# One drain a step in place of raises on PE's products, in a message-passing layer of a graph network

## The chip, the core and the metric

The kernel runs on one core of a Trainium2 chip. It has five engines with a queue each, which work side by side: PE (TensorE) multiplies matrices, DVE (VectorE) and ACT (ScalarE) do elementwise work, POOL (GpSimd) here issues gathers, and SP (SyncE) issues other transfers. An engine waits for another by a semaphore, which an instruction raises when it completes. The metric is the device time of one execution in microseconds. PE's granted clock is listed by the profile as a share of full speed.

## The reference

The inputs are 12,500 nodes `x` with 128 numbers each, and 400,000 edges with a source, a destination (sorted) and a distance. What is computed, cut to what matters:

```python
rbf = exp(-(d[:, None] - centers) ** 2 / (2 * width * width))   # 50 centers
cut = 0.5 * (cos(pi * d / 10) + 1) * (d <= 10)
W = (silu(rbf @ fw1 + fb1) @ fw2 + fb2) * cut[:, None]
messages = (h[src] @ pw + pb) * W
agg = segment_sum(messages, dst, num_segments=num_atoms)
h1 = h + (silu(agg @ mw1 + mb1) @ mw2 + mb2)
out = layernorm(x + h1, axis=-1)
```

The distances are scaled so that most edges lie beyond the cutoff and contribute nothing.

## The kernel before

**Stages.** First the nodes are projected (`h @ pw + pb`) into a table `proj` in HBM, four blocks of 128 at a time (helpers at L1003, L345, L348), while the edges are packed in seven chunks: DVE drops those beyond the cutoff and lists source, destination and factor of the rest. Then a loop goes over 139 quads of edges; a quad is four tiles of 128 edges, 512 in all. The steps 0 to 131 stand in one loop, the last ones are written out by hand. Node blocks are finished in between, as soon as their edges have been summed, and later chunks are still packed in the first steps.

**One step q of the loop.** The order in which the code names the operations is the order of each engine's queue:

- `message(q)`, DVE, L1201: the filter of quad q (a PSUM bank `pu`) times the gathered rows gives `msg`, 128 x 512.
- `nodes(q)`: work on finished node blocks; `node_first` (PE L1282, L1283, then ACT L1285 into `zs`), `node_second` (PE L345, L348), statistics (DVE L1320, L1324), normalisation (ACT L1371).
- Gathers of the rows of later quads, POOL, L1099, four a quad. A table PACE says at which count of DVE's vector instructions each is issued, so they are spread among DVE's work.
- `second(q + 2)`, PE, L1182 and L1185: bias and four products with `fw2` into a bank.
- In steps with q%4 of 0 and 1: `first(octs(q))`, PE, L1167, two products of 512 columns into `ph`, and `silu(octs(q))`, ACT, L1173, from `ph` into `s`. One such pair serves two quads, four and five or six and seven steps after the group's first; `ph` is a single buffer of two banks, `s` has three.
- In steps with q%4 of 3: two `basis`, ACT, L1151 (square) and L1155 (exponential), into `rbf` (two buffers). Silu and exponential need different tables, so ACT loads a table ahead of the first of each pair.
- `sum_up(q)`, PE, L1235: four products of `msg` with the column matrices `hot` into `sums`, two PSUM buffers for two quads each.
- `place(q + 1)`, DVE, L1214: four column matrices `hot` of the next quad, from destinations and cutoff factors. `msg` and `hot` have two buffers up to quad 65, four from 66 on (`own`).
- `add`, DVE, L1269: the sums of an earlier pair of quads are added into `aggT` at an address that is loaded first (L1244).

An fp32 product runs on PE as two passes, so one product of L1185 or L1235 stands as two instructions in the profile, with a weight load each.

**What sets the waits.** A scheduler finds for each instruction what it depends on, and gives it a wait on the semaphore of the engine that made it. Any product of PE that somebody waits for raises PE's semaphore (PE_49 in the listings below). The tiles `rbf`, `ph` and `s` are taken from a pool that turns their buffers.

Of the kernel before, what the change touches and what calls it, by code (L numbers as in the profile page):

```python
# [29 lines left out]
QT = 4  # L30
# [25 lines left out]
OTHERS = 4, 5, 6, 7  # L56
OWN_4 = 66
DIRECT = 32
FIRST = 16
LISTS = 5  # L60
PACE = ((2, 17), (3, 26), (4, 36), (5, 54), (7, 95), (9, 125), (10, 144), (12, 170), (18, 250), (24, 324), (30, 373), (36, 458), (42, 544), (48, 612), (54, 691), (60, 754), (66, 826), (72, 902), (78, 982), (84, 1071), (90, 1139), (96, 1218), (102, 1306), (108, 1357), (114, 1414), (120, 1461), (126, 1518), (132, 1580), (138, 1646), (139, 1666))
# [30 lines left out]
def kernel(  # L92
# [288 lines left out]
        return max([int(DONE[0] * max(p - s, 0) ** 2) - 1] + [n for k, n in LAST.items() if p >= k])  # L381
    proj = nc.dram_tensor("proj", [N, H], F32).ap()
    near_d = nc.dram_tensor("near_d", [NP, 2 * P], F32).ap()

    free = [ps.tile([P, 512], F32, name=f"bank{k}", bufs=1) for k in range(4)]
    held = []
# [445 lines left out]
    def unpack(c):  # L832
# [14 lines left out]
            listed(pair, a, b, 0, 3)  # L847
        if c < 2:
            more_ = np_ if c == 0 else SPILL
            also = work.tile([P, 2, QE], F32, name="s", bufs=3).bitcast(I32)  # L850
            listed(also, 0, more_, 3, LISTS)
        awake[c] = max(awake[c], clock[0]) + (6 if c < 1 else 3.5 if c < 2 else 4.0)
        yield 0
# [172 lines left out]
        free.append(b)  # L1026


    d_of, rbf_of, ph_of, t_of, s_of, pu_of, got_of, pa_of, hot_of = ({} for _ in range(9))


# [55 lines left out]
    def beside(n):  # L1087

        while n and singles[1]:
            n -= 1  # L1090
            one_row(1)
# [48 lines left out]
    def basis(o):  # L1140
        if o not in d_of:
            for q in quads(o):
                while chunk_of(q) not in stored:
                    go_on(todo[0])
            radials(o + 1)
        d, n = d_of.pop(o)
        u = 2 * KR
        rbf = work.tile([P, QE], F32, name="rbf")
        if o >= 0:
            nc.scalar.wait_ge(d_sem[o % 3], 16 * (o // 3 + 1))  # L1150
        a = nc.scalar.activation(rbf[:u], d[:u], AF.Square, bias=rbf_bias[:u], scale=rbf_scale[:u])  # L1151
        if o >= 0:
            tc.declare_no_dep(a.ins, group="lengths", reason="waits on d_sem")
        beside(HIDE[0])
        nc.scalar.activation(rbf[:u], rbf[:u], AF.Exp, scale=-1.0 / (2.0 * width * width))  # L1155
        beside(HIDE[1])
        rbf_of[o] = rbf, n
        if o >= 0:
            based[0] = o + 1
            radials(o + 4)  # L1160

    def first(o):

        rbf, n = rbf_of.pop(o)
        ph = ps.tile([P, 2, QE], F32, name="ph", bufs=1)
        for h in range(n):
            nc.tensor.matmul(ph[:, h, :], w1_sb[:2 * KR, h, :], rbf[:2 * KR], start=True, stop=True)  # L1167
        ph_of[o] = ph, n

    def silu(o):  # L1170
        ph, n = ph_of.pop(o)
        s = work.tile([P, 2, QE], F32, name="s", bufs=3)
        nc.scalar.activation(s[:, :n], ph[:, :n], AF.Silu)  # L1173
        beside(HIDE[2])
        for h in range(n):
            s_of[2 * o + h] = s[:, h]

    def second(q):

        s = s_of.pop(q)  # L1180
        pu = bank()
        nc.tensor.matmul(pu, ones_b[:, :P], bias_b["fb2"].rearrange("k j f -> k (j f)"), start=True,  # L1182
                         stop=False)
        for j in range(QT):
            nc.tensor.matmul(pu[:, j * H:(j + 1) * H], s[:, j * P:(j + 1) * P], fw2_sb,  # L1185
                             start=False, stop=(j == QT - 1))
        pu_of[q] = pu

    def message(q, js=(0, QT)):
        gathers(q + 1)  # L1190
        msg = own(q, "msg", 0)
        a, b = js
        if q in SINGLY and a == 0:
            act = q in BY_ACT
            k = (BY_ACT if act else BY_SP).index(q)
            assert q in alone and all(s[0] != q for s in singles[act])
            nc.vector.wait_ge(row_sem[act][k % ROW_SEMS], 16 * P * (k // ROW_SEMS + 1))
            m = nc.vector.tensor_mul(msg[:, 0, :], pu_of[q][:, :H], alone.pop(q))
            tc.declare_no_dep(m.ins, group="rows", reason="waits on row_sem")
            a = 1  # L1200
        nc.vector.tensor_mul(msg[:, a:b, :], pu_of[q].rearrange("p (j f) -> p j f", j=QT)[:, a:b, :],  # L1201
                             got_of[q][:, a:b, :])
        if b == QT:
            free.append(pu_of.pop(q))
            got_of.pop(q)
        gathers()
        return msg

    def place(q):

        hot = own(q, "hot", 1)
        for j in range(QT):
            at = 2 * q + j // 2, slice(j % 2, j % 2 + 1)
            nc.vector.tensor_scalar(hot[:, j, :wide(q)], iota_n[:, :wide(q)], dl[:, at[0], at[1]],  # L1214
                                    cut[:, at[0], at[1]], op0=OP.is_equal, op1=OP.mult)
            gathers()
        hot_of[q] = hot

# [8 lines left out]
    def sum_up(q, msg, js=range(QT)):  # L1227
        hot = hot_of[q]
        if q % 2 == 0 and 0 in js:
            pa_of["two"] = ps.tile([P, 2, 2 * W], F32, name="sums", bufs=2)  # L1230
        pa = pa_of[q] = pa_of["two"][:, q % 2, :]
        n = QT // windows(q)
        for j in js:
            k = j // n
            nc.tensor.matmul(pa[:, k * W:k * W + wide(q)], msg[:, j, :], hot[:, j, :wide(q)],  # L1235
                             start=(j % n == 0), stop=(j % n == n - 1))

    bases = {}

# [25 lines left out]
    def add(q, ks=(0, 1)):  # L1265
        pa = pa_of[q]
        for k in ks[:windows(q)]:
            to = aggT[:, ds(bases.pop((q, k)), wide(q))]
            nc.vector.tensor_add(to, to, pa[:, k * W:k * W + wide(q)])  # L1269
            gathers()  # L1270
        done[0] = q + (ks[-1] == 1)

# [179 lines left out]

    def keep_busy(n):

        ph = ps.tile([P, 2, QE], F32, name="ph", bufs=1)
        for k in range(n):
            nc.tensor.matmul(ph[:, k % 2, :], ones_b[:, :P],
                             bias_b["mb2"].rearrange("k j f -> k (j f)"), start=True, stop=True)
# [132 lines left out]

    some, counted = None, []
    for q in range(NL - 7):
        while todo and q + 2 >= DIRECT // QT and todo[0] <= chunk_of(min(q + 2, NQ - 1)):
# [12 lines left out]
        radials(q // 2 + 5)  # L1607
        one_by_one()
        multiplies(q + 1 + EARLY_X)
        if q + 2 < NL:  # L1610
            second(q + 2)
        if q % 4 < 2 and 2 * octs(q) < NL:
            first(octs(q))
            silu(octs(q))
        if q % 4 == 3:
            for o in (q // 4 * 2 + 4, q // 4 * 2 + 5):
                if 2 * o < NL and q < NL - 8:
                    basis(o)
        sum_up(q, msg)
        now = range(added(q), added(q + 1))  # L1620
        at_once = len(now) == 2 and wide(now[0]) == wide(now[1]) and windows(now[0]) == windows(now[1])
        if at_once:
            bases_of(list(now))
        else:
            for k in now:
                base_of(k, (0,))
        place(q + 1)
        for k in now:
            if not at_once:
                base_of(k, (1,))  # L1630
            add(k)
        tail(q)
        clock[0] = max(clock[0], there_at[q])
        summed[q] = clock[0] + 0.7
        clock[0] += 2.2 + 0.3 * (windows(q) - 1)
        if q == 0:
            clear_packed(2, nc.sync)
        if todo:
            pack_until(max(there_at[q + 1], clock[0] + (PACK_US if known[0] >= QB[3] else EARLY_US)), NC_)
        if NODES - 8 <= q < NODES - 2:  # L1640
            part_of(*(("mb1", mb1_f) if q < NODES - 5 else ("mb2", mb2_f)), (q - NODES + 8) % 3)
        if not todo and not counted:
            counted.append(q)
            count()
        elif counted and some is None and fetched[0] >= QT * NL and not queue:
            some = nc.values_load(bad_i[0:1, 2:3], min_val=0, max_val=3 * E)
    def house(q):
# [247 lines left out]
```

## Time and profile before

| | us |
|---|---|
| median of three runs | 956.14 |
| the runs | 954.89, 956.14, 960.9 |
| the profiled execution | 950.38 |
| its span | 948.8 |
| PE busy in it | 663.7 |
| POOL busy in it | 539.2 |
| granted clock of PE in it | 0.808 of full speed |

The span is the time from the first to the last instruction of the profiled execution. Rows of groups give line, engine, operation, tile, shape and count, then the busy time in us and the mean of one in ns, then the idle time of the engine ahead of them with what ended it. "remote" there is a wait that ended with a semaphore's event at which the profile finds no instruction of this core that had just ended; in the chain the same is called "another core or an unknown queue". "issue" is time in which an engine waited for nothing that the profile shows. Rows of the timeline give the start, the duration, the engine and line, and in brackets the idle time before.

### The profile page before, as it was taken

The numbers are of one execution on the slowest core, as the hardware profiler recorded it, in microseconds if no ns is written. First come the engines' busy times: TensorE is split into PE (matmuls) and PEld (weight loads), VectorE is DVE, ScalarE is ACT, GpSimd is POOL, SyncE is SP. The second block draws the span as 40 slices with busy tenths as digits, with TensorE's granted clock in tenths as the row PEclk, the third lists the DMA queues.
The fourth block names the chain that finished last, engine by engine and source line by source line (L and its number), as shares of the span: only waits on it lengthen the run. The fifth ranks groups of instructions, "written<-read, shape, count | busy, mean of one in ns | idle before, by whom it ended". The sixth has DMA issues, their size and how long they took to land.

```text
span 948.8 us, 11718 instructions
## 1 busy us (share of the span) xinstructions
PE 663.7 (70%) x3531; PEld 517.3 (55%) x3531; DVE 565.9 (60%) x1725; ACT 398.0 (42%) x567; POOL 539.2 (57%) x577
## 2 busy tenths in 40 slices
PE   4663737749778867767767786868796675777656
PEld 3552535537556755655555564646575554554444
DVE  8356638745778767767678584646553344443536
ACT  4432622316335443534334433634643542454235
POOL 6346355565556656666666465546565566664661
PEclk8677767778778878888978898769987787778778
DMA  7574421232233223232324122432422342232222
GB/s 243 161 222 154 147 96 34 77 92 81 62 79 120 71 62 82 69 108 77 94 64 136 54 68 67 120 100 67 142 63 63 105 122 67 65 111 81 70 75 74
DMA packets 51295, 91.23 MB, mean 96 GB/s; under 512 B 12928, under 2 KB 18656, under 8 KB 51226
## 3 DMA queue, kind: packets, MB, share of 16 engines
q0 software_dynamic: 18096, 37.30, 15.6%
q1 hardware_dynamic: 22868, 35.09, 11.2%
q10 hardware_dynamic: 10262, 18.05, 6.0%
q8 instruction: 29, 0.48, 0.2%
q14 instruction: 40, 0.33, 0.1%
HBM read 74.59 MB, written 15.79 MB: 95 GB/s over the span
## 4 chain that ended last, share of the span: by engine, by line
PE 42%; another core or an unknown queue 16%; issue 13%; DVE 13%; ACT 10%; DVEq 1%; DMA 1%; ACTq 0%
PE ph L1167 11%; PE bank L1185 9%; PE sums L1235 9%; PE bank L348 5%; DVE hot L1214 3%; PE bank L1182 3%; PE bank L1283 2%; DVE msg L1201 2%; ACT s L1173 2%; ACT rbf L1151 2%; PE bank L1003 1%; PE bank L345 1%; ACT rbf L1155 1%; DVE aggT L1269 1%
## 5 line engine op out<-in xcount | busy, mean ns | idle before, releaser
L1099 POOL DMA_INDIRECT quad<-proj,srci x412 | 391.7, 951 | 274.0 <-issue 86.1
L1185 PEld LDWEIGHTS bank<-fw_sb,s 128*128 128x128 f32 x1112 | 177.1, 225 | 90.2 <-issue 83.6
L1173 ACT ACTIVATE s<-ph 128x1024 f32<-128x1024 f32 x70 | 71.2, 1017 | 335.6 <-PE ph L1167 159.9
L1167 PE MATMUL ph<-rbf,w_sb 102*128 102x512 f32 x278 | 164.1, 719 | 51.7 <-ACT s L1173 35.7
L1185 PE MATMUL bank<-fw_sb,s 128*128 128x128 f32 x1112 | 180.1, 310 | 22.5 <-issue 22.2
L1214 DVE TENSOR_SCALAR hot<-iota_n,dl,cut 128x80 f32<-128x80 f32 (+4 forms) x408 | 111.1, 338 | 107.0 <-PE sums L1235 49.6
L1235 PEld LDWEIGHTS sums<-hot,msg 128*128 128x128 f32 x816 | 121.5, 218 | 61.3 <-issue 40.3
L1235 PE MATMUL sums<-hot,msg 128*128 128x80 f32 (+4 forms) x816 | 122.5, 299 | 17.3 <-DVE msg L1201 10.1
L1099 POOL DMA_INDIRECT x<-proj,srci x96 | 91.4, 952 | 66.4 <-issue 21.3
L1167 PEld LDWEIGHTS ph<-rbf,w_sb 102*128 102x128 f32 x278 | 57.3, 229 | 99.7 <-issue 58.8
L1269 DVE TENSOR_TENSOR aggT<-aggT,sums 128x80 f32 (+4 forms) x209 | 53.9, 258 | 94.1 <-remote 33.8
L1182 PE MATMUL bank<-fb_b,ones_b 96*128 96x512 bf16 x139 | 60.3, 434 | 49.6 <-DVE msg L1201 15.2
L1201 DVE TENSOR_TENSOR msg<-bank,quad 128x512 f32<-128x512 f32 x78 | 53.2, 682 | 46.2 <-remote 32.7
L348 PEld LDWEIGHTS bank<-pw_sb,xT 128*128 128x128 f32 (+1 forms) x292 | 47.2, 232 | 59.0 <-issue 40.3
L1099 POOL DMA_INDIRECT quad<-in_x_dram,srci x48 | 46.3, 965 | 33.9 <-issue 12.6
L1235 PE MATMUL sums<-quad,quad 128*128 128x128 f32 (+3 forms) x296 | 49.4, 309 | 15.8 <-issue 15.2
L1151 ACT ACTIVATE rbf<-d_sb,rbf_bias,rbf_scale 102x512 f32<-102x512 f32 x70 | 56.1, 801 | 0.0
L1235 PEld LDWEIGHTS sums<-quad,quad 128*128 128x128 f32 x296 | 45.0, 225 | 20.1 <-issue 18.8
L348 PE MATMUL bank<-pw_sb,xT 128*128 128x128 f32 (+1 forms) x292 | 48.5, 319 | 6.2 <-ACT xT L1005 5.6
L345 PE MATMUL bank<-pb_b,ones_b 96*128 96x512 bf16 (+2 forms) x38 | 16.8, 443 | 46.4 <-ACT xT L1005 29.0
L1201 DVE TENSOR_TENSOR quad<-bank,quad 128x512 f32<-128x512 f32 (+1 forms) x40 | 25.9, 647 | 38.0 <-DMA quad<-proj,srci 24.2
L1005 ACT COPY xT<-bank 128x512 f32<-128x512 f32 (+1 forms) x37 | 21.3, 580 | 63.5 <-remote 49.0
(278 smaller groups left out, 881.7 us busy)
## 6 DMA issues: line engine op xcount, KB each, us to landing
d_sb<-near_d ACTq DMA_DIRECT2D x67, 256.0 KB
x<-in_x_dram SPq DMA_DIRECT2D x46, 256.0 KB
quad<-proj,srci POOLq DMA_INDIRECT x412
proj<-hp SPq DMA_DIRECT2D x24, 256.0 KB
out_dram<-x SPq DMA_DIRECT2D x22, 256.0 KB
x<-proj,srci POOLq DMA_INDIRECT x96
r_d<-in_edge_weight_dram SPq DMA_DIRECT2D x5, 256.0 KB
r_dst<-in_dst_dram SPq DMA_DIRECT2D x5, 256.0 KB
```

The source lines that it names most:

```text
L345: nc.tensor.matmul(to[:m, a:a + c, :], ones_b[:, :m], bias_b[:, :c, :], start=True, stop=False)
L348: nc.tensor.matmul(to[:m, k, :], lT[:, k * P:k * P + m], w, start=False, stop=(k == a + c - 1))
L1099: g = nc.gpsimd.indirect_dma_start(out=got[:, j, :], out_offset=None, in_=proj if table is None else table, in_offset=bass.IndirectOffsetO ...
L1151: a = nc.scalar.activation(rbf[:u], d[:u], AF.Square, bias=rbf_bias[:u], scale=rbf_scale[:u])
L1167: nc.tensor.matmul(ph[:, h, :], w1_sb[:2 * KR, h, :], rbf[:2 * KR], start=True, stop=True)
L1173: nc.scalar.activation(s[:, :n], ph[:, :n], AF.Silu)
L1182: nc.tensor.matmul(pu, ones_b[:, :P], bias_b["fb2"].rearrange("k j f -> k (j f)"), start=True, stop=False)
L1185: nc.tensor.matmul(pu[:, j * H:(j + 1) * H], s[:, j * P:(j + 1) * P], fw2_sb, start=False, stop=(j == QT - 1))
L1201: nc.vector.tensor_mul(msg[:, a:b, :], pu_of[q].rearrange("p (j f) -> p j f", j=QT)[:, a:b, :], got_of[q][:, a:b, :])
L1214: nc.vector.tensor_scalar(hot[:, j, :wide(q)], iota_n[:, :wide(q)], dl[:, at[0], at[1]], cut[:, at[0], at[1]], op0=OP.is_equal, op1=OP.mult)
L1235: nc.tensor.matmul(pa[:, k * W:k * W + wide(q)], msg[:, j, :], hot[:, j, :wide(q)], start=(j % n == 0), stop=(j % n == n - 1))
L1269: nc.vector.tensor_add(to, to, pa[:, k * W:k * W + wide(q)])
```

## The change

From step 4 on the products of `first`, `second` and `sum_up` are left out of the scheduler's dependences and raise nothing. Behind each step's `sum_up` PE gets a `drain` that raises a semaphore `products` by one: 128 of them, for the steps 4 to 131. Those who read what the products wrote, or write what the products read, wait for a count of that semaphore, an engine only once for each count. `message(q)` waits for the drain of step q - 2, where its `second` was issued. `place(q + 1)` waits for the drain of the last step that read the buffer. `add` waits for the later step of its pair, `basis` for step q - 2. `silu` is moved behind `sum_up` and the drain, and waits for the drain of its own step. Since dependences are no longer tracked on them, `s`, `rbf` and `ph` become fixed buffers taken in turn. The node blocks, the packing, the projection and the steps written by hand keep their raises. In the built programs the products that raise fall from 601 to 251. PE's order of products is the same.

```diff
+    pe_sem = tc.alloc_semaphore("products")
+    step_q, waited = [-1], {}
+
+    def drained():
+
+        d = nc.tensor.drain()
+        d.then_inc(pe_sem, 1)
+        tc.no_tile_sem_insts.add(d.ins.name)
+
+    def product(i):
+
+        if step_q[0] >= FROM_DRAIN:
+            tc.add_to_no_dep_group("products", i.ins)
+
+    def behind(eng, q):
+
+        n = q - FROM_DRAIN + 1
+        if step_q[0] < 0 or n <= 0:
+            return False
+        if n > waited.get(str(eng.engine), 0):
+            waited[str(eng.engine)] = n
+            eng.wait_ge(pe_sem, n)
+        return True
+
+    def no_word(i, on=True):
+
+        if on:
+            tc.declare_no_dep(i.ins, group="products", reason="the engine waited on pe_sem")
...
     def silu(o):
         ph, n = ph_of.pop(o)
-        s = work.tile([P, 2, QE], F32, name="s", bufs=3)
-        nc.scalar.activation(s[:, :n], ph[:, :n], AF.Silu)
+        s = in_turn_of("s", [P, 2, QE], 3)
+        known_q = behind(nc.scalar, step_q[0])
+        no_word(nc.scalar.activation(s[:, :n], ph[:, :n], AF.Silu), known_q)
...
     def message(q, js=(0, QT)):
         gathers(q + 1)
         msg = own(q, "msg", 0)
         a, b = js
+        known_q = behind(nc.vector, q - 2)
...
     def place(q):
 
         hot = own(q, "hot", 1)
+        known_q = behind(nc.vector, q - (4 if q >= OWN_4 + 4 else 2))
...
             to = aggT[:, ds(bases.pop((q, k)), wide(q))]
-            nc.vector.tensor_add(to, to, pa[:, k * W:k * W + wide(q)])
+            known_q = behind(nc.vector, min(q | 1, step_q[0]))
+            no_word(nc.vector.tensor_add(to, to, pa[:, k * W:k * W + wide(q)]), known_q)
...
             second(q + 2)
         if q % 4 < 2 and 2 * octs(q) < NL:
             first(octs(q))
-            silu(octs(q))
         if q % 4 == 3:
             for o in (q // 4 * 2 + 4, q // 4 * 2 + 5):
                 if 2 * o < NL and q < NL - 8:
                     basis(o)
         sum_up(q, msg)
+        if q >= FROM_DRAIN:
+            drained()
+        if q % 4 < 2 and 2 * octs(q) < NL:
+            silu(octs(q))
```

On ACT a group of four steps reads as follows before; the two silus are those of its first and second step, and L237 clears a piece of `aggT`:

```order
L237 ACTIVATE aggT<-iota_n 128x500 [waits DVE_49]
L1173 ACT_TABLE_LOAD
L1173 ACTIVATE s<-ph 128x1024 [waits PE_49]
L237 ACTIVATE aggT<-iota_n 128x500
L1173 ACTIVATE s<-ph 128x1024 [waits PE_49]
```

The same place on ACT after the change, where L1173 has become L1217:

```order
L238 ACTIVATE aggT<-iota_n 128x500 [waits DVE_49]
L1217 ACT_TABLE_LOAD [waits products]
L1217 ACTIVATE s_560<-ph_958 128x1024
L238 ACTIVATE aggT<-iota_n 128x500
L1217 ACTIVATE s_961<-ph_958 128x1024 [waits products]
```

The waits of both silus are on the new semaphore, and at the first the wait has moved ahead of the table load; so it stands at 23 of the 32 loads that belong to a changed silu, and at the others between load and silu.

On DVE a step of the chunk whose columns are 112 wide reads as follows before; the message is L1201, the columns L1214, and the two additions L1269, with address instructions between them:

```order
L1201 TENSOR_TENSOR msg_680<-bank_170,quad_84 128x512 [waits DMASW3_49,DMASW4_49,DMASW2_49,DMASW1_49]
L1244 TENSOR_LOAD base_i
L1214 TENSOR_SCALAR hot_1073<-iota_n,dl,cut 128x112 [waits PE_49] x4
L1269 ISA
L1269 TENSOR_TENSOR aggT<-aggT,sums 128x112
L1269 ISA
L1269 TENSOR_TENSOR aggT<-aggT,sums 128x112 [waits DVE_49]
```

The same step on DVE after the change:

```order
L1247 TENSOR_TENSOR msg_680<-bank_170,quad_84 128x512 [waits DMASW3_49,DMASW4_49,DMASW2_49,DMASW1_49]
L1295 TENSOR_LOAD base_i
L1263 TENSOR_SCALAR hot_1069<-iota_n,dl,cut 128x112 [waits products]
L1263 TENSOR_SCALAR hot_1069<-iota_n,dl,cut 128x112 x3
L1321 ISA
L1321 TENSOR_TENSOR aggT<-aggT,sums 128x112
L1321 ISA
L1321 TENSOR_TENSOR aggT<-aggT,sums 128x112 [waits DVE_49]
```

The four column matrices waited each for one product of the sums that had read their slice; now the first waits for a drain and the rest for nothing. Message and additions have no wait of their own on PE at this place, before or after.

More of the change, by code (lines that the diff above doesn't have):

```diff
@@ L58 @@
 DIRECT = 32
+FROM_DRAIN = 4
 FIRST = 16
@@ L383, with in_turn_of @@
     near_d = nc.dram_tensor("near_d", [NP, 2 * P], F32).ap()
+    turn_of = {}
+    def in_turn_of(name, shape, n, pool=keep):
+        k = turn_of[name] = turn_of.get(name, -1) + 1
+        if k < n:
+            turn_of[name, k] = pool.tile(shape, F32, name=f"{name}{k}", bufs=1)
+        return turn_of[name, k % n]
     free = [ps.tile([P, 512], F32, name=f"bank{k}", bufs=1) for k in range(4)]
@@ L849, in unpack @@
             more_ = np_ if c == 0 else SPILL
-            also = work.tile([P, 2, QE], F32, name="s", bufs=3).bitcast(I32)
+            also = in_turn_of("s", [P, 2, QE], 3).bitcast(I32)
             listed(also, 0, more_, 3, LISTS)
@@ L1147, in basis @@
         u = 2 * KR
-        rbf = work.tile([P, QE], F32, name="rbf")
+        rbf = in_turn_of("rbf", [P, QE], 2)
         if o >= 0:
             nc.scalar.wait_ge(d_sem[o % 3], 16 * (o // 3 + 1))
+        known_q = behind(nc.scalar, step_q[0] - 2)
         a = nc.scalar.activation(rbf[:u], d[:u], AF.Square, bias=rbf_bias[:u], scale=rbf_scale[:u])
@@ L1153, in basis @@
             tc.declare_no_dep(a.ins, group="lengths", reason="waits on d_sem")
+        no_word(a, known_q)
         beside(HIDE[0])
-        nc.scalar.activation(rbf[:u], rbf[:u], AF.Exp, scale=-1.0 / (2.0 * width * width))
+        no_word(nc.scalar.activation(rbf[:u], rbf[:u], AF.Exp, scale=-1.0 / (2.0 * width * width)),
+                known_q)
         beside(HIDE[1])
@@ L1164, in first @@
         rbf, n = rbf_of.pop(o)
-        ph = ps.tile([P, 2, QE], F32, name="ph", bufs=1)
+        ph = in_turn_of("ph", [P, 2, QE], 1, ps)
         for h in range(n):
-            nc.tensor.matmul(ph[:, h, :], w1_sb[:2 * KR, h, :], rbf[:2 * KR], start=True, stop=True)
+            product(nc.tensor.matmul(ph[:, h, :], w1_sb[:2 * KR, h, :], rbf[:2 * KR], start=True,
+                                     stop=True))
         ph_of[o] = ph, n
@@ L1181, in second @@
         pu = bank()
-        nc.tensor.matmul(pu, ones_b[:, :P], bias_b["fb2"].rearrange("k j f -> k (j f)"), start=True,
-                         stop=False)
+        product(nc.tensor.matmul(pu, ones_b[:, :P], bias_b["fb2"].rearrange("k j f -> k (j f)"),
+                                 start=True, stop=False))
         for j in range(QT):
-            nc.tensor.matmul(pu[:, j * H:(j + 1) * H], s[:, j * P:(j + 1) * P], fw2_sb,
-                             start=False, stop=(j == QT - 1))
+            product(nc.tensor.matmul(pu[:, j * H:(j + 1) * H], s[:, j * P:(j + 1) * P], fw2_sb,
+                                     start=False, stop=(j == QT - 1)))
         pu_of[q] = pu
@@ L1199, in message @@
             tc.declare_no_dep(m.ins, group="rows", reason="waits on row_sem")
+            no_word(m, known_q)
             a = 1
-        nc.vector.tensor_mul(msg[:, a:b, :], pu_of[q].rearrange("p (j f) -> p j f", j=QT)[:, a:b, :],
-                             got_of[q][:, a:b, :])
+        m = nc.vector.tensor_mul(msg[:, a:b, :],
+                                 pu_of[q].rearrange("p (j f) -> p j f", j=QT)[:, a:b, :],
+                                 got_of[q][:, a:b, :])
+        no_word(m, known_q)
         if b == QT:
@@ L1211, in place @@
         hot = own(q, "hot", 1)
+        known_q = behind(nc.vector, q - (4 if q >= OWN_4 + 4 else 2))
         for j in range(QT):
             at = 2 * q + j // 2, slice(j % 2, j % 2 + 1)
-            nc.vector.tensor_scalar(hot[:, j, :wide(q)], iota_n[:, :wide(q)], dl[:, at[0], at[1]],
+            i = nc.vector.tensor_scalar(hot[:, j, :wide(q)], iota_n[:, :wide(q)], dl[:, at[0], at[1]],
                                     cut[:, at[0], at[1]], op0=OP.is_equal, op1=OP.mult)
+            no_word(i, known_q)
             gathers()
@@ L1234, in sum_up @@
             k = j // n
-            nc.tensor.matmul(pa[:, k * W:k * W + wide(q)], msg[:, j, :], hot[:, j, :wide(q)],
-                             start=(j % n == 0), stop=(j % n == n - 1))
+            product(nc.tensor.matmul(pa[:, k * W:k * W + wide(q)], msg[:, j, :],
+                                     hot[:, j, :wide(q)], start=(j % n == 0),
+                                     stop=(j % n == n - 1)))
     bases = {}
@@ L1453, in keep_busy @@
     def keep_busy(n):
-        ph = ps.tile([P, 2, QE], F32, name="ph", bufs=1)
+        ph = in_turn_of("ph", [P, 2, QE], 1, ps)
         for k in range(n):
@@ L1646 @@
             some = nc.values_load(bad_i[0:1, 2:3], min_val=0, max_val=3 * E)
+    step_q[0] = -1
     def house(q):
```

1 line of the change is left out of this document (added).

## The prediction

> **What bounds the kernel now.** I read the page first: engines, then the chain that ended last.
>
> ```profile
> span 948.8 us, 11718 instructions
> PE 663.7 (70%) x3531; PEld 517.3 (55%) x3531; DVE 565.9 (60%) x1725; ACT 398.0 (42%) x567; POOL 539.2 (57%) x577
> PE 42%; another core or an unknown queue 16%; issue 13%; DVE 13%; ACT 10%; DVEq 1%; DMA 1%; ACTq 0%
> ```
>
> No engine is full. PE carries 42% of the chain, and 16% is time for which the profile finds no cause on this one core. The change lies in the steps of the loop, so I asked for the chain from 165 to 925 us, and for the bias products of `second` (one a step) in that stretch.
>
> ```profile
> by line: another core or an unknown queue 17.4%; PE ph L1167 12.9%; issue 12.5%; PE bank L1185 11.3%; PE sums L1235 10.3%; DVE hot L1214 3.7%; PE bank L1182 3.1%; PE bank L348 2.5%; PE bank L1283 2.3%; DVE msg L1201 2.3%; ACT s L1173 1.8%;
> 165.00:925.00 760.00, 57.02 (x132) 16.97 (x132) 0.82 0.30 85
> ```
>
> 132 steps in 760 us are 5.76 us a step. Of the chain there PE has 12.9 + 11.3 + 10.3 + 3.1 + 2.5 + 2.3 = 42.4%: what I add to PE's time counts, as an estimate, with 0.424. The unexplained 17.4% are 0.174 x 760 = 132 us. The list of waits tells who stands in it (columns: total us, times, longest).
>
> ```profile
> ACT s L1173 <- remote: 109.2, 14, 11.9
> DVE hot L1214 <- remote: 44.9, 18, 5.3
> DVE aggT L1269 <- remote: 33.8, 7, 6.7
> DVE msg L1201 <- remote: 32.7, 6, 8.3
> ```
>
> All four wait for PE's semaphore in the code, so "remote" here is a raise that came when no product of PE had just ended: 14 + 18 + 7 + 6 = 45 times. One of them in the timeline, about 608 us:
>
> ```profile
> 608.68 1.88 PE L1167 MATMUL ph<-rbf,w_sb 102*128 102x512 f32 x4
> ...
> 621.74 0.94 POOL L1099 DMA_INDIRECT quad<-proj,srci  x1 [0.31 <-issue]
> 623.24 1.02 ACT L1173 ACTIVATE s<-ph 128x1024 f32<-128x1024 f32 x1 [11.04 <-remote]
> ...
> 626.19 0.94 POOL L1099 DMA_INDIRECT quad<-proj,srci  x1 [3.51 <-DVE base L954]
> ```
>
> `first` was through at 610.56; its silu began at 623.24, 12.7 us later and 0.6 us behind the end of a gather, after which POOL paused for 3.5 us. So PE's word is late while gathers follow each other. The question on which the forecast turns is whether only the word is late, or the product's completion. A second place says something on that:
>
> ```profile
> 782.01 1.05 PE L348 MATMUL bank<-mw_sb,zs 128*128 128x128 f32 x8
> 782.90 0.38 PE L1182 MATMUL bank<-fb_b,ones_b 96*128 96x512 bf16 x1
> 783.12 1.05 PE L1185 MATMUL bank<-fw_sb,s 128*128 128x128 f32 x8
> 784.01 1.06 PE L1235 MATMUL sums<-quad,quad 128*128 128x128 f32 x8
> 784.91 0.38 PE L1182 MATMUL bank<-fb_b,ones_b 96*128 96x512 bf16 x1
> 785.13 1.18 PE L1185 MATMUL bank<-fw_sb,s 128*128 128x128 f32 x6
> 787.96 0.27 PE L1185 MATMUL bank<-fw_sb,s 128*128 128x128 f32 x1 [1.65 <-issue]
> 790.08 0.37 PE L1185 MATMUL bank<-fw_sb,s 128*128 128x128 f32 x1 [1.85 <-issue]
> 792.18 0.37 PE L1235 MATMUL sums<-quad,quad 128*128 128x128 f32 x1 [1.72 <-issue]
> 793.37 0.94 POOL L1099 DMA_INDIRECT quad<-proj,srci  x1 [0.30 <-issue]
> 794.97 0.37 PE L1235 MATMUL sums<-quad,quad 128*128 128x128 f32 x1 [2.42 <-issue]
> 797.07 1.44 PE L1235 MATMUL sums<-quad,quad 128*128 128x128 f32 x6 [1.73 <-issue]
> ```
>
> From 787.96 PE starts one pass every 2.1 us, waiting for no engine, and runs freely again behind POOL's pause. Between the first L348 pass and the one at 787.96 lie 8 + 1 + 8 + 8 + 1 + 6 = 32 passes. I read this as a window: a pass starts only when the one 32 before it has retired. Those that retired so slowly are then the passes of L348, and the first seven of these raise nothing. So completion itself seems late, raise or not.
>
> **The change, part by part.** In the two programs the products that raise fall from 601 to 251; 128 drains that raise are added, one a step from step 4 to 131. Their order among PE's other instructions is unchanged, as are POOL and SP.
>
> *Raises taken away: 0.* A stretch at full clock shows what a raise costs PE, and gives the prices for the drain and for `silu`:
>
> ```profile
> 499.79 1.08 PE L1235 MATMUL sums<-hot,msg 128*128 128x112 f32 x8
> 500.60 0.11 PEld L1182 LDWEIGHTS <-ones_b 96*128 96x128 bf16 x1
> 500.71 0.38 PE L1182 MATMUL bank<-fb_b,ones_b 96*128 96x512 bf16 x1
> 500.93 1.05 PE L1185 MATMUL bank<-fw_sb,s 128*128 128x128 f32 x8
> 501.82 1.88 PE L1167 MATMUL ph<-rbf,w_sb 102*128 102x512 f32 x4
> 503.54 1.04 PE L1235 MATMUL sums<-hot,msg 128*128 128x112 f32 x8
> 503.74 1.02 ACT L1173 ACTIVATE s<-ph 128x1024 f32<-128x1024 f32 x1 [1.72 <-issue]
> 506.07 1.15 PE L1235 MATMUL sums<-quad,quad 128*128 128x112 f32 x8 [0.38 <-DVE quad L1201]
> 509.39 0.69 DVE L1201 TENSOR_TENSOR quad<-bank,quad 128x512 f32<-128x512 f32 x1
> ```
>
> The eight passes of L1185 take from 500.93 to the start of `first` at 501.82, 0.11 us each, with the raise on the last; the next product follows at the same 0.11 us. So I take 0 for 350 raises. The Trainium skill, TensorE: Matmul & The Clock Gate, section "The cost: per-tile semaphore tail", says that such increments are written one behind the other at about 26.3 ns each; by it 350 fewer would be an estimated 9 us less work, and the sum below about 980 instead of 989. These rows don't show it in PE's pace.
>
> *Drains: +21.* A drain keeps the next product back until the sums have ended. Back to back, L1182 starts at 500.71, 0.16 us before the modelled end of the sums (499.79 + 1.08). Behind a drain this 0.16 is lost; the weight load of 0.11 us, hidden now, stands open; and a group that starts from rest takes 1.15 instead of 1.04, 0.11 more. That is 0.38 us, times 128 = 49 us on PE, times 0.424 = 21. Bounds: 0 where PE waits anyway after the sums, and twice the price at half clock with all of it on the path, 97 us. A drain alone gains nothing. I take the middle since the three parts come from rows of just this place.
>
> *`silu` behind sums and drain: +12.* At 503.74 the silu starts 0.04 us after `first` ended, while the sums run. Now it waits for them (1.04) and the drain. `ph` is one buffer: the next step's `first` must wait for that silu. Half of the silus are preceded by a table load, and in the new order the wait stands ahead of 23 of these loads:
>
> ```profile
> L1173 ACT ACT_TABLE_LOAD x35 | 44.9, 1283 | 0.8 <-issue 0.2
> PE ph L1167 <- ACT s L1173: 35.7, 9, 6.6
> ```
>
> Behind the drain come load and silu, 1.28 + 1.02 = 2.30 us; PE has only `second` to fill it, 501.82 - 500.71 = 1.11. PE stands 1.2 us, 23 times: 28 us, times 0.424 = 12. In the nine other steps with q%4 = 0 the load comes ahead of the wait, and 1.02 us fit under 1.11. The silus with q%4 = 1 are needed three steps on: 0. Before, this wait occurred 9 times in all; it should become some 30. Bounds: 0 if the step waits for its rows anyway, 28 if all of it counts. What is queued behind the waiting silu on ACT is the node blocks' work and the basis of a later step, both with a step or more in hand.
>
> *Message, columns, additions, basis: 0.* A message waited for its `second`, now for the drain of that step. `second` ended at 501.98, the sums of its step at 503.54 + 1.04 = 504.58, and its message came at 509.39: the word comes 2.6 + 0.4 us later than now, and 4.4 us are left. Up to step 69 the message has no wait of its own: the columns of the step ahead have waited for the same drain. The columns waited for the last sums from their buffer, one step back (three with four buffers), now for the drain right behind: 0.4 us later, on an engine 60% busy. The additions take sums two steps old, the basis a drain two steps old. If the cover is gone, each costs the drain's 0.4 us a step, inside the drain's upper bound.
>
> *The late word: 0.* If completion is late, the drain is late too, and the 132 us stay. Bounds: -132 to +50 (below).
>
> Sum: 21 + 12 = 33 on the profiled run's own 950.4 us (its span is 948.8), so 983. The median of the runs, 956.14, lies 5.8 above this one: **989 us**.
>
> **The rivals.** *Faster: the word alone is late.* If PE's raises queue up somewhere while gathers are issued, one raise a step in place of two or three shortens that queue. With half of the 132 us gone, the node blocks' and chunks' raises remaining, it is 989 - 66 = 923. It decides from 33 us, 25% of the stall. For it: the waits above are for raises, and "remote" says that no product ended then. Against it: the passes 2.1 us apart. The Trainium skill, PSUM — Partial Sum Buffer, section "Engine vs sequencer instructions", says that a drain waits until the engine is fully idle; no run here shows a drain yet, but by that rule one behind a late product is as late.
>
> *No change: gathers set the pace.*
>
> ```profile
> L1099 POOL DMA_INDIRECT quad<-proj,srci x412 | 391.7, 951 | 274.0 <-issue 86.1
> POOL quad L1099 <- DVE hot L1214: 56.5, 42, 6.9
> ```
>
> A gather takes 0.95 us plus 0.30 between: 1.25, and four are 5.0 of a step's 5.76 us, while PE's own step is 2.0 us, or 3.75 with `first` (1.11 for `second`, 503.54 - 501.82 = 1.72, and 500.71 - 499.79 = 0.92 for the sums). Then both terms are hidden: 956. Against it: POOL itself waits for the columns, 56.5 us.
>
> *Worse: no run ahead.* In the 45 late places PE now goes on for up to 32 passes. Behind a late drain it can't. If each loses one `second`, 1.11 us, that is 50 more: 1039.
>
> That the change does nothing is excluded by the new waits in the queues of ACT and DVE.
>
> **How the numbers follow.** Forecast (966 to 1012 as its own range) 0.36; worse 0.13; no change 0.18; faster 0.33, since the evidence on completions is one reading of few rows. About 1% is what a measurement of this kernel can tell from no change. So faster by over 1% 0.33, within 1% 0.18, slower 0.49. The range goes from 915, where 56% of the stall is gone, to 1035, short of the worse case's middle; some 0.1 is left out at each end.
>
> **What would show it.** The share of PE in the chain of the loop should rise, and bias products after the sums should show a gap near 0.4 us, waiting for no engine. `ph` should wait for the silu some 30 times. "Remote" waits of silu, columns and messages should stay near 220 us in all (109.2 + 44.9 + 33.8 + 32.7). The forecast is wrong if they fall by half: then the word was late, not the product. It is also wrong if gathers stay 5.0 us a step with POOL waiting less, so that the gaps cost nothing.

## The result and the profile after

The changed kernel took 1002.23 us in the median (997.26 to 1004.98, four runs) beside 955.51 for the kernel before: a ratio of 1.056, with an interval from 1.050 to 1.062. The ratio is worked out from fast runs alone and is not that of the two medians, 1.049: by it the loss would be some 53 us, by the medians it is 47. Forecast were 989. The profiled execution took 1002.41, with a span of 1000.9 and a granted clock of 0.806, the same as before (0.808).

The page of the changed kernel: span, busy times, and the chain that ended last.

```profile
span 1000.9 us, 11857 instructions
PE 694.7 (69%) x3531; PEld 536.3 (54%) x3531; DVE 565.1 (56%) x1725; ACT 398.3 (40%) x567; POOL 540.5 (54%) x577
issue 26%; PEld 24%; PEldq 15%; PE 14%; DVE 8%; ACT 6%; another core or an unknown queue 5%; DMA 0%; DVEq 0%; SPq 0%; ACTq 0%
```

The work is the same. The unexplained share fell from 16% to 5%, and in its place stands PEldq with 15%: that is PE's sequencer, L1044, the drain. "issue" has doubled. So the stall has not gone; it has been given a name. The list of waits of the changed kernel says where it stands (total us, times, longest):

```profile
ACT L1217 <- PEq L1044: 220.1, 23, 13.6
ACT s L1217 <- PEq L1044: 179.9, 37, 10.5
PEld L1226 <- issue: 123.3, 90, 8.4
PE bank L1226 <- issue: 106.1, 36, 8.2
DVE hot L1263 <- PEq L1044: 105.1, 40, 8.8
DVE quad L1247 <- PEq L1044: 48.3, 8, 8.4
DVE msg L1247 <- PEq L1044: 32.4, 10, 6.9
PE ph L1209 <- ACT s L1217: 13.1, 15, 1.1
```

The two rows of L1247 are both messages, whose buffer is named `msg` in the one and `quad` in the other. L1226 is the bias product of `second`, the first thing that PE does behind a drain in 67 of the 128 steps. It stood without a named cause for 106.1 us in 36 places. The same wait in the kernel before:

```profile
PE bank L1182 <- issue: 9.1, 10, 2.6
```

That is the drains' main mark: nearly 100 us more in which PE stands ahead of this product and waits for no engine. In the timeline of the changed kernel one such place looks like this:

```profile
512.52 1.04 PE L1285 MATMUL sums<-hot,msg 128*128 128x112 f32 x8
...
516.67 0.95 POOL L1138 DMA_INDIRECT quad<-proj,srci  x1 [0.30 <-issue]
519.55 1.08 DVE L1263 TENSOR_SCALAR hot<-iota_n,dl,cut 128x112 f32<-128x112 f32 x4 [3.77 <-PEq L1044]
519.57 0.60 PE L1226 MATMUL bank<-fb_b,ones_b 96*128 96x512 bf16 x1 [6.00 <-issue]
...
520.41 1.04 POOL L1138 DMA_INDIRECT quad<-proj,srci  x1 [2.79 <-DVE hot L1263]
```

The sums were through at 513.56 by the model of their ends. Gathers followed each other until 517.62, and 1.9 us after the last of them the drain ended: the columns on DVE and the next product on PE both start there, 6.0 us late. POOL then waits for the columns, since its gathers are paced by DVE's count. I set the end of each of the 128 drains against the modelled end of the last product before it: 79 end within 0.1 us of it, 46 more than 0.5 us behind it (168.8 us in all, 9.7 at most). In 20 of these 46 places no product between the drain before and this one raises anything. So it is not only a raise that is late there.

### The profile page after: what moved, and what is told of

It is laid out like the page before. It is cut to its first block, busy times and chain, and to the rows that moved or that the text cites. A ratio compares the mean times of both kernels' runs of the same rounds, so it can differ in the third digit from the quotient of the medians.

```text
span 1000.9 us, 11857 instructions
## 1 busy us (share of the span) xinstructions
PE 694.7 (69%) x3531; PEld 536.3 (54%) x3531; DVE 565.1 (56%) x1725; ACT 398.3 (40%) x567; POOL 540.5 (54%) x577
## 4 chain that ended last, share of the span: by engine, by line
issue 26%; PEld 24%; PEldq 15%; PE 14%; DVE 8%; ACT 6%; another core or an unknown queue 5%; DMA 0%; DVEq 0%; SPq 0%; ACTq 0%
PEldq L1044 15%; PEld sums L1285 9%; PEld bank L1229 9%; PE bank L349 4%; PEld bank L349 2%; PE ph L1209 2%; PEld ph L1209 2%; ACT s L1217 2%; ACT L1217 2%; PE bank L1229 2%; PE sums L1285 2%; PE bank L1013 1%; DVE hot L1263 1%; PE bank L346 1%
## 5 line engine op out<-in xcount | busy, mean ns | idle before, releaser
L1229 PEld LDWEIGHTS bank<-fw_sb,s 128*128 128x128 f32 x1112 | 189.7, 241 | 38.7 <-issue 31.2
L1229 PE MATMUL bank<-fw_sb,s 128*128 128x128 f32 x1112 | 189.1, 326 | 0.0
L1209 PE MATMUL ph<-rbf,w_sb 102*128 102x512 f32 x278 | 169.7, 741 | 18.3 <-ACT s L1217 13.1
L1263 DVE TENSOR_SCALAR hot<-iota_n,dl,cut 128x80 f32<-128x80 f32 (+4 forms) x408 | 108.0, 335 | 130.1 <-PEq L1044 105.1
L1217 ACT ACTIVATE s<-ph 128x1024 f32<-128x1024 f32 x70 | 71.2, 1017 | 209.9 <-PEq L1044 179.9
L1226 PE MATMUL bank<-fb_b,ones_b 96*128 96x512 bf16 x139 | 64.0, 460 | 126.4 <-issue 106.1
L1217 ACT ACT_TABLE_LOAD x35 | 44.9, 1283 | 220.3 <-PEq L1044 220.1
L1209 PEld LDWEIGHTS ph<-rbf,w_sb 102*128 102x128 f32 x278 | 59.8, 239 | 70.0 <-issue 50.1
L1226 PEld LDWEIGHTS <-ones_b 96*128 96x128 bf16 x139 | 14.8, 107 | 124.2 <-issue 123.3
L1247 DVE TENSOR_TENSOR msg<-bank,quad 128x512 f32<-128x512 f32 x78 | 53.2, 683 | 48.3 <-PEq L1044 32.4
L1247 DVE TENSOR_TENSOR quad<-bank,quad 128x512 f32<-128x512 f32 (+1 forms) x40 | 25.9, 647 | 75.4 <-PEq L1044 48.3
L1285 PE MATMUL sums<-quad,quad 128*128 128x128 f32 (+3 forms) x296 | 45.6, 303 | 1.2 <-DVE quad L1247 1.1
```

What stands on the lines that cost most here:

```text
L1209: product(nc.tensor.matmul(ph[:, h, :], w1_sb[:2 * KR, h, :], rbf[:2 * KR], start=True, stop=True))
L1217: no_word(nc.scalar.activation(s[:, :n], ph[:, :n], AF.Silu), known_q)
L1226: product(nc.tensor.matmul(pu, ones_b[:, :P], bias_b["fb2"].rearrange("k j f -> k (j f)"), start=True, stop=False))
L1229: product(nc.tensor.matmul(pu[:, j * H:(j + 1) * H], s[:, j * P:(j + 1) * P], fw2_sb, start=False, stop=(j == QT - 1)))
L1247: m = nc.vector.tensor_mul(msg[:, a:b, :], pu_of[q].rearrange("p (j f) -> p j f", j=QT)[:, a:b, :], got_of[q][:, a:b, :])
L1263: i = nc.vector.tensor_scalar(hot[:, j, :wide(q)], iota_n[:, :wide(q)], dl[:, at[0], at[1]], cut[:, at[0], at[1]], op0=OP.is_equal, op1=OP ...
```

## The experiments

The runs fell on several chips, and this turned out to matter more than any edit. On two of them the kernel before takes 954 to 955 us, as at first; on two others 736 to 737. A ratio is always taken to the kernel before on the same chip. The first measurement, with 955.5, is of the first kind. No chip is known to have been met in two sessions, so "kind of chip" may also be the state that a chip was in at the time.

**The drain by itself.** The kernel before, with a drain behind the sums and nothing else:

```diff
         sum_up(q, msg)
+        if q >= 4:
+            tc.no_tile_sem_insts.add(nc.tensor.drain().ins.name)
```

> The kernel before with a drain behind the sums of the steps 4 to 131 that raises nothing and that nobody waits for; every raise and wait of before stays, silu too. Theory A (a drain holds PE back where completions are late, so PE loses its run ahead): +30 to +45 us on before's 955, that is 985 to 1000. Theory B (each drain has a fixed price of 0.2 to 0.4 us on PE, the rest of the loss is silu's): +10 to +21, 965 to 976. Theory C (the loss is the moved silu alone): within 1% of before.

Measured: 1003.59 us beside 954.14, ratio 1.051 (1.044 to 1.059). A drain that nobody waits for costs 49 us, about as much as the whole change. That is 3.6 us above theory A's range and far from B's and C's. Its timeline shows what it takes away, and more:

```profile
501.97 1.15 PE L1235 MATMUL sums<-hot,msg 128*128 128x112 f32 x8
...
506.91 0.95 POOL L1099 DMA_INDIRECT quad<-proj,srci  x1 [0.30 <-issue]
508.16 0.94 POOL L1099 DMA_INDIRECT quad<-proj,srci  x1 [0.30 <-issue]
508.21 0.34 DVE L1214 TENSOR_SCALAR hot<-iota_n,dl,cut 128x112 f32<-128x112 f32 x1 [1.56 <-remote]
510.37 0.34 DVE L1214 TENSOR_SCALAR hot<-iota_n,dl,cut 128x112 f32<-128x112 f32 x1 [1.82 <-remote]
...
511.11 0.61 PE L1182 MATMUL bank<-fb_b,ones_b 96*128 96x512 bf16 x1 [7.99 <-issue]
```

The products still raise here, so their completions are seen one by one: the columns at 508.21 and 510.37 go into the buffer that these very sums read, and get the word of its last two products 2.2 us apart, though the model has all of them through at 503.12. The drain ends behind the second of these words, and PE stands for 8 us. Without a drain PE goes on with the next step in most such places. In the steps that have a drain, the time from the start of the last pass of a step's sums to the start of PE's next product is over 1 us in 12 places before (32 us in all) and in 49 with the drain (230 us).

**The place of `silu` by itself.** The kernel before, with the call moved behind the sums:

```diff
             first(octs(q))
-            silu(octs(q))
...
         sum_up(q, msg)
+        if q % 4 < 2 and 2 * octs(q) < NL:
+            silu(octs(q))
```

> The kernel before with silu moved behind the sums in the code, with no drain; it still waits for the raise of its own products. It takes its place on ACT, and its wait has not moved to a later product. Theory A and B: within 1% of before, at most +5 us. Theory C: +30 us or more, above 985.

Measured: 955.08 beside 954.14, ratio 0.9998 (0.997 to 1.003). The order in the code costs nothing, as all theories but C had it. Then the other way round, the changed kernel with `silu` and its word where they were:

```diff
         for h in range(n):
-            product(nc.tensor.matmul(ph[:, h, :], w1_sb[:2 * KR, h, :], rbf[:2 * KR], start=True,
-                                     stop=True))
+            nc.tensor.matmul(ph[:, h, :], w1_sb[:2 * KR, h, :], rbf[:2 * KR], start=True, stop=True)
...
-        known_q = behind(nc.scalar, step_q[0])
+        known_q = behind(nc.scalar, step_q[0] - 2)
...
             first(octs(q))
+            silu(octs(q))
```

> The changed kernel with silu at its old place right behind its products, which raise again, as many as before; drains, their raises and the other waits stay. Theory A: 0 to 10 us below the changed kernel, 992 to 1002. Theory B: 12 below or somewhat more, 985 to 990. Theory C: within 1% of before, 946 to 965.

Measured: 983.27 beside 954.14, ratio 1.031 (1.025 to 1.036). This is 29 us over before, against 45 to 47 for the full change, measured on other chips: the later word of `silu` is worth some 17 us where there are drains (by the ratios of the full change, 1.056 and 1.051, it would be 19 to 24). Theory A had 0 to 10 for it, B 12 or somewhat more; the time itself is far below A's range and 2 us below B's. C falls by this run and the last.

**The word without the hold.** In place of each drain a weight load raises the semaphore; it goes in PE's order, but PE may start what comes behind it:

```diff
+    word = nc.alloc_sbuf_tensor("word", [P, P], BF16).ap()
+    nc.vector.memset(word, 0.0)
...
-        d = nc.tensor.drain()
+        d = nc.tensor.ldweights(word)
         d.then_inc(pe_sem, 1)
```

> The changed kernel with a weight load of 128 columns in place of each drain; the load raises the same semaphore, and nothing holds PE back behind it. Silu stays late and waits for it. Theory A: the loss of the drains goes, silu's 0 to 12 us stays: 955 to 967. Theory B: a load of 0.11 us in place of 0.2 to 0.4 us: 975 to 990. Theory C: 985 to 1002. If it ends below before, fewer raises do help once PE is not held back.

Measured: 969.33 beside 954.14, ratio 1.012 (1.006 to 1.019). This is 2 us above theory A's range and 6 below B's. About 32 of the change's 47 us go with the hold. The 15 left (12 by the ratio) are near what `silu`'s later word cost above; that they are the same was not shown, since the run that could tell met a chip without late completions (below). The waits of this run:

```profile
ACT L1219 <- remote: 88.7, 11, 13.6
ACT s L1219 <- remote: 63.2, 10, 8.5
PE ph L1211 <- ACT s L1219: 61.7, 21, 8.0
DVE hot L1265 <- remote: 48.1, 14, 6.6
DVE msg L1249 <- remote: 46.3, 8, 9.6
DVE aggT L1323 <- remote: 26.1, 6, 8.1
PE bank L1228 <- issue: 9.5, 12, 2.0
```

L1228 is the bias product again: 9.5 us, as before. The late word itself is still there: the "remote" waits of silu, columns, messages and additions are 272 us, where the same rows were 221 before. So a raise that needs no empty PE is late all the same, and it is not the number of raises that makes it late: this kernel has as few as the changed one. PE waits for `silu` 21 times, 61.7 us, where before it was 9 times and 35.7 us.

One thing speaks against the load as a word. In this trace each of the 128 loads ends 0.11 to 0.6 us before the modelled end of the last product ahead of it, and readers that it releases start up to 0.39 us before that end. So the run gives the price of a word without a hold; that the products are through when it comes is not shown.

**What makes completions late.** The next four kernels ran on one chip, of the second kind. The first has POOL's gathers replaced by transfers of fixed rows, issued by SP, the second has the drains on top:

```diff
-            i = srci[:, 2 * q + j // 2, j % 2:j % 2 + 1] if idx is None else idx[:, j:j + 1]
-            g = nc.gpsimd.indirect_dma_start(
-                out=got[:, j, :], out_offset=None, in_=proj if table is None else table,
-                in_offset=bass.IndirectOffsetOnAxis(ap=i, axis=0))
+            r = (37 * abs(q) + 53 * j) % 90 * P
+            g = nc.sync.dma_start(out=got[:, j, :], in_=(proj if table is None else table)[r:r + P])
```

> The kernel before with each gather replaced by a direct transfer of 128 rows of the same table at a fixed place, issued by SP; POOL issues no gathers, and the rows of the edges are not the right ones. If gathers in flight make completions late (theory A's ground), the late waits of silu, columns and messages, 221 us before, fall under 50 us, and the time falls below 925. If they are late for another reason, these waits stay above 150 us.

> The same with the 128 drains that raise nothing. Theory A (the drains cost by late completions): nearly all drains end within 0.1 us of the last sums, and the drains add 5 to 20 us to the run without them. Theory B' (a drain costs its 49 us whatever the gathers do): 35 us or more on top of the run without drains.

Measured: 661.45 and 675.76 beside 737.49, ratios 0.899 (0.893 to 0.906) and 0.916 (0.914 to 0.918). The drains add 14 us here, all 128 on time, as theory A had it. But the kernels with gathers that were profiled on this chip (the next two) have no late word either: no wait of theirs ends "remote". So the pair doesn't tell what the gathers do to completions. It does give the fixed price: with PE busy 87% of the span, 128 drains cost 14 us.

The third put the drain ahead of the sums instead of behind them:

```diff
+        if q >= 4:
+            tc.no_tile_sem_insts.add(nc.tensor.drain().ins.name)
         sum_up(q, msg)
```

> The kernel before with a drain that raises nothing ahead of the sums of the steps 4 to 131 instead of behind them. Theory A: the completions of second and first are late as well there, so +30 to +50, 985 to 1005. Theory D (the loss comes from the place, behind which second could have run ahead; ahead of the sums PE often waits for the message anyway): +5 to +25, 960 to 980.

Measured: 735.9 beside 737.49, ratio 0.999 (0.997 to 1.001), all 128 drains on time. Both theories assumed late completions, of which there were none; that place was not tried on a chip of the other kind.

The fourth joined the raising load with `silu`'s old place:

> The changed kernel with the raising weight load in place of the drain, and silu back behind its products, which raise as before. Theory A: silu's later word is what is left of the load run's 14 us, so within 1% of before, 946 to 965. A rival: the one word for message and columns, one step's rest later, costs them: 965 to 975. Below 946 would mean that fewer raises help.

Measured: 737.96, ratio 0.999 (0.997 to 1.001). No loss and no gain; with nothing late, fewer raises bring nothing that shows. Neither forecast could be tried, since both were for late completions.

Two more runs, on another chip, where before took 954.74:

> The changed kernel once more, beside a run of the kernel before, since the last four runs met a chip on which before takes 737 us, PE's clock is 0.93 and no drain ended late. Theory A (the loss is late completions that a drain makes PE wait for): where drains are on time, the change costs no more than 0 to 10 us; where they are late, 40 to 55 again. Theory B (the fixed price and silu's order): 20 to 35 us on either chip.

> The kernel before with direct transfers issued by SP in place of POOL's gathers, and the 128 drains that raise nothing; the rows are not those of the edges. On a chip where gathers go with late completions: if gathers cause them, fewer than 5 of 128 drains end over 0.5 us behind the last sums; if the chip does, 40 or more as with the gathers. On a chip without late completions: none, and it tells nothing.

Measured: the changed kernel 999.72, ratio 1.051 (1.041 to 1.061), 45 of 128 drains over 0.5 us late, 171 us in all. On the same chip the kernel with direct transfers and drains had none late, and took 670.4 us in its one run, with PE's clock at 0.947. So late completions belong to POOL's gathers, on such a chip: without them it took what the other kind took (675.76). This rests on one run.

The last two runs met the other kind again:

> The changed kernel with the raising weight load in place of the drain, and silu at its old place, once more, since its first run met the chip without late completions (there within 0.2% of before). Where completions are late, before is about 955. Theory A: 946 to 965, since nothing holds PE back and silu's word is as early as before. The rival (message and columns pay for the one word a step): 965 to 975, as with silu late. Below 946: fewer raises help.

> The changed kernel beside it. Theory A: 40 to 55 us above before where completions are late (two chips so far), 0 to 10 us above it where they are not (before 737 us). Theory B: 20 to 35 us on either.

Measured: the load with `silu`'s old place 735.93 beside 736.07, ratio 1.000 (0.999 to 1.002), and the changed kernel 736.33, ratio 1.001 (0.999 to 1.003). The change that costs 45 to 47 us on one kind of chip costs nothing on the other. That is as theory A had it, and theory B, with 20 to 35 us on either, falls. What its page and lists show there:

```profile
span 732.9 us, 11857 instructions
PE 594.8 (81%) x3531; PEld 456.4 (62%) x3531; DVE 561.3 (77%) x1725; ACT 396.9 (54%) x567; POOL 540.1 (74%) x577
L1138 POOL DMA_INDIRECT quad<-proj,srci x412 | 391.4, 950 | 130.7 <-issue 54.6 <-DVE aggT L1321 13.1 <-DVE msg L1247 10.3
ACT L1217 <- PEq L1044: 123.2, 23, 9.6
PE ph L1209 <- ACT s L1217: 15.3, 14, 1.8
```

All 128 drains end within 0.1 us of the sums. The drains and the waits behind them are there, PE waits for `silu` as often as on the first kind (14 times, 15.3 us). But POOL goes from gather to gather: its idle time before the 412 of them is 130.7 us, 0.32 each, which is hardly more than the 0.30 between gathers that follow at once; in the kernel before on the slower kind it was 274.0. At 0.95 us each the gathers take just as long on both. So they seem to set the pace and to hide the price on PE. The runs on the second kind fit this: without POOL's gathers the time falls from 737 to 661, and only then do the drains show, with 14 us.

## Why the prediction was right

The direction and, within a factor, the size came out: +33 forecast, +47 measured, inside the range. The step on which it turned, that completion itself is late, is borne out. The size is in part luck: of the terms one was far too small, and one that was put at nothing made up for much of it. And on a chip of the second kind the forecast would have failed. By its steps:

- *The late word stays (0), since completion itself is late.* This was the hinge, and it holds. The drains end late in 46 of 128 places, in 20 of them behind products that raise nothing, and a raise on a load is late too. The rule of the Trainium skill, PSUM — Partial Sum Buffer, section "Engine vs sequencer instructions", that a drain waits for a fully idle engine, agrees with the drain that ended 6.0 us behind the sums. The rival in which only the word is late, and fewer raises shorten the queue, falls: with the same 251 raising products and no hold, the load run was not below before but 15 us above it, and its "remote" waits had grown from 221 us to 272. In the changed kernel itself this sign can't be read, since a late wait there stands under the drain's name.
- *Drains, +21.* The fixed price was put too high, and the term was too small all the same. Between rows as in the forecast, sums to next bias product took 0.92 us, and behind a prompt drain of the changed kernel (529.70 to 530.82 in the rows below) 1.12: 0.20 instead of the 0.38 that I added up. Over the whole trace the median from the start of the last pass of the sums to the next product is 0.36 us behind the prompt drains and 0.11 before, so 0.24 or 0.25 each. But on this kind of chip the drain alone costs 49 us, since PE stands wherever completions are late. That was my rival "no run ahead", priced at 50 us on top of the forecast with a chance of 0.13. The counts agree (45 late waits before, 46 late drains), but the 45 are waits of four readers and were not matched with steps, so this may be chance. The price of a place was not the 1.11 us of the forecast: the late drains end 3.7 us late on average. What the rival adds is about 49 less the fixed price (14 us in the pair with direct transfers), not 50 beyond all the rest. It belonged into the sum.
- *Raises taken away, 0.* With `silu` in its old place the change costs 29 us, and the drain alone 49, though that kernel keeps all raises and waits. So few raises and one word a step give back some 20 us where there are drains (ratios 1.031 and 1.051, intervals apart). I had 0. Which of the two gives it was not separated. In the one trace of each, the late drains add up to 212 us of lateness in the kernel with the drain alone and 184 with `silu` in its old place. Without drains no gain was seen: 0.999 and 1.000, and those only where nothing is late. The 26.3 ns a raise of the Trainium skill, TensorE: Matmul & The Clock Gate, section "The cost: per-tile semaphore tail", an estimated 9 us, shows in neither.
- *`silu`, +12.* Measured some 17, or more by the ratios. The mechanism is there as described: drain, table load, silu, then `first`.

```profile
525.50 1.28 ACT L1217 ACT_TABLE_LOAD   x1 [10.67 <-PEq L1044]
525.71 1.06 PE L1229 MATMUL bank<-fw_sb,s 128*128 128x128 f32 x8
526.80 1.02 ACT L1217 ACTIVATE s<-ph 128x1024 f32<-128x1024 f32 x1
527.88 1.98 PE L1209 MATMUL ph<-rbf,w_sb 102*128 102x512 f32 x4 [1.11 <-ACT s L1217]
529.70 1.04 PE L1285 MATMUL sums<-hot,msg 128*128 128x112 f32 x8
530.82 0.39 PE L1226 MATMUL bank<-fb_b,ones_b 96*128 96x512 bf16 x1
```

  PE stands 1.1 us at 527.88 as forecast (1.2). But there are 15 such waits with 13.1 us, not 30 with 28; with `silu` in its old place there is one, with 0.8 us. So 12 us more of PE's time stand here, and this alone doesn't carry 17. Nor did the wait grow against the kernel before, where it was 35.7 us in 9 places: with the drain alone it is 0.8 us too, since PE then stands at the drain instead. What is left of the 17 may be the later word elsewhere: the load waits 220.1 us for drains in 23 places, and a drain that is late holds `silu` back where its own products' word would have come first. That is argued; no run separates it.
- *Message and columns, 0.* Their waits did grow. By all rows of the lists that end with PE or "remote", the columns waited 103 us before and 125 after, the messages 46 and 81. But with the drain alone, which nobody waits for, it is already 121 and 68. So the word once a step adds some 17 us of waiting in all; what that costs was not measured by itself, and is part of the -20 of the term above.
- *The rival "gathers set the pace"* is what seems to happen on the other kind of chip, with the result that it gave: no change.
- *The signs.* PE's share of the chain did not rise: PE and its weight loads have 14 + 24 = 38% of it after, over the whole execution, and had 42% before, and the drain has 15% besides. The gap behind the sums is there, nearer to 0.25 us than to 0.4.

So the sum of the steps, 21 + 12 + 0, stood for 49 + 17 - 20 = 46. These three are differences between runs, so they add up to the measured loss by construction; they show where it arises, not that each cause is understood.

## What to carry to other kernels

A drain costs PE about 0.25 us where completions are prompt, and that may hide. Where completions are late it takes away PE's run ahead, and its price is then the lateness, not the instruction; so look first whether words of PE come late ("remote" waits, single passes a constant time apart) before putting a drain, or anything else that waits for an empty engine, into a loop. A word that PE need not stop for costs less, but what it says of the products ahead of it must be settled first. And a change to such a kernel should be timed on more than one chip: here the same edit is worth 5% on one and nothing on the next.

## What the runs showed of the hardware

- The same program takes 955 us on two chips and 737 on two others, each with narrow spread. What differs in the traces of the changed kernel is lateness (45 and 46 late drains of 128 on the first kind, none on the second) and the granted clock. On the first kind PE's completions lag while gathers issued by POOL follow each other, by up to 12.7 us in the forecast's example. Single gathers take as long on both (951 and 950 ns).
- On the slower kind it goes away with the gathers: with direct transfers and drains 670 us, none late. What in such a chip links POOL's gathers to PE's completions stays open.
- The granted clock goes along: 0.80 to 0.81 in the profiled executions with late completions, 0.92 to 0.95 in those without, and 0.947 on the slower kind once the gathers were gone. Whether it is a cause or follows from PE's pauses was not tried.
- In the two late places shown, completions come one at a time: 2.1 us apart for passes in the forecast's rows, and 2.2 us apart for words in the drain's run.
